# Selective scans: four of sixteen input products per job made by scaling a transposed tile and turning it back (two in layer 1)

## The chip, the core and the metric

The kernel runs on one core of a Trainium2 chip. The metric is the device time of one execution in microseconds, lower is better. A core has five engines that run side by side, each with its own queue of instructions in a fixed order: PE (TensorE: matmuls and transposes, writes to PSUM only), DVE (VectorE), ACT (ScalarE), POOL (GpSimd), and SP, which here issues the DMAs.

## What is computed

The program is four layers on a tensor of 2 images x 56 x 56 positions x 128 channels (L = 3136 positions): two state-space layers, then an attention with a long-filter mixer, then an attention with experts. The change is in the first two, in their selective scans. Cut to what matters:

```python
def step(state, inp):                      # one position after another
    u_i, d_i, b_i, c_i = inp
    dA = jnp.exp(d_i[..., None] * A)       # decay, per channel d and state n (N = 16)
    state = dA * state + (d_i * u_i)[..., None] * b_i[:, :, None, :]
    y = jnp.einsum('bkdn,bkn->bkd', state, c_i)
    return (state, y)
```

There are four directions k: along the rows, along the columns, and both backwards. `delta` d is a softplus of a small projection, B and C are projections as well, the same for all channels. Layer 0 has 256 channels per image, so two tiles of 128 channels, and handles one image after the other. Layer 1 is called for four "heads" in turn with 64 channels per image, so both images share one tile of 128 partitions.

## The kernel before

Class `Scans` (from line 111) does the scans of both layers. The positions are cut into four quarters of 784. A group is one direction and one quarter (16 groups); a job is a group and one channel tile (`ci`); a job has 16 steps, one for each state n. Layer 0 has 32 jobs per image, layer 1 has 16 per head: 2048 steps in all. Channels lie on the partitions, positions along the free dimension, so one step is a handful of 128x784 instructions:

- the decay a = exp(A delta), by ACT into one of two PSUM slots, `pa`, that alternate by step (line 339)
- the input product h = du x B, where du = delta x input (line 223), and B has one row per state that all partitions need. There are two kinds of it. For a pooled state (`POOLED`, five of 16: 2, 5, 8, 11, 14) a DMA broadcasts the row from DRAM to all partitions (line 299, tile `b`), and POOL multiplies (line 433). For the other eleven PE spreads the row with two bf16 matmuls into the single PSUM tile `pb` (line 364), and DVE multiplies (line 417)
- the scan itself by DVE, h = a h_before + h, in place (line 358)
- the product p = h x C by POOL, with C broadcast by DMA (lines 299 and 430)
- the sum over states by PE: matmuls with the identity (layer 1: a centering matrix) that accumulate in PSUM (`add_up`, line 378). A job's accumulation opens with `begin_sum` (line 392) and ends with `take_out` by ACT (line 398).

The order is written out by hand: `emit(s)` issues what belongs to step s, and the scheduler is off (`manual_schedule`). In one `emit(s)`, in this order: decay of step s+1; the state of s-1 saved (`keep`, line 350); DVE's product of s+1; PE's spread for s+2; pieces of preparation at place 0; the scan of s; DMA of B for s+6 and of C for s+3; POOL's p of s, then POOL's product of s+3; the sums; pieces at place 2. The sums are opened when step n = 2 of a job is two steps old; after that each step adds one product, and the steps n = 6, 9 and 12 add two.

The preparation of the next group is cut into pieces, and `preparation` (line 257) says at which step and place each goes: `rows` (projection by PE, copy by ACT), `keep`, `fetch`, `band`, `rest`, `store` and `spread` (B split into three bf16 parts, by way of DRAM), `steps` (delta's projection), `soft` (softplus, which needs another ACT table), `copy` (the input by PE into PSUM, with an identity matmul) and `times` (du by DVE). Pieces of place 0 take the PSUM tile `pb` too. The first group of each run of scans is prepared by `first` (line 230), which is called in the stage before, at the third of its seven chunks.

Tiles h and p have six buffers each, C four, B two.

Of the kernel before, what the change touches and what calls it, by code (L numbers as in the profile page):

```python
# [106 lines left out]
POOLED = (2, 5, 8, 11, 14)  # L107
HALF = QT // 2


class Scans:
# [13 lines left out]
    def __init__(self, k, ctx, nch, row, col, y, w, side=None):  # L125
# [7 lines left out]
        )  # L133

    def begin(self):
        self.groups = []
        for kd in (0, 2, 1, 3):
            back = kd >= 2
            for step, q in enumerate(range(4) if not back else range(3, -1, -1)):
                self.groups.append(dict(kd=kd, q=q, step=step, back=back))  # L140

    def open(self, ctx):
        k, nch = self.k, self.nch
        self.once = ctx.enter_context(k.pool("scan4", 1))
        self.two = ctx.enter_context(k.pool("scan5", 2))
        self.hp = ctx.enter_context(k.pool("scanh", 6))
# [8 lines left out]
    def pieces_of(self, g, once, dram):  # L155
# [60 lines left out]
        def copy(ci, ps):  # L216
            g["copy"] = product(ps, [0, 1], lambda m: k.ident, [xq[ci]])

        def times(ci, copied=True):
# [4 lines left out]

        return dict(
            rows=rows, keep=keep, fetch=fetch, band=band, rest=rest, store=store, spread=spread, steps=steps,
            soft=soft, copy=copy, times=times,
        )

    def first(self, pool):  # L230

        self.begin()
        own = {"xd": self.y[0][:, 0:QT], "whole": self.y[-1][:, QT : QT + QT // 4]}
# [20 lines left out]
        for ci in range(self.nch):  # L254
            f["times"](ci, False)

    def preparation(self, groups, short):
# [15 lines left out]
        if self.nch == 2:  # L273
            lists = [[
                (0, 0, "rows", [0]), (3, 0, "rows", [1]), *bands(5, 8, 11, 2, 16, 19), (12, 0, "steps", 0, [0, 1]),
                (16, 0, "steps", 1, [0, 1]), (20, 2, "soft", 0), (20, 2, "soft", 1), *du(22, 0), *du(25, 1),
            ]]
        elif short:
            lists = [
                [(0, 0, "rows", [0, 1]), *bands(1, 3, 5, 1, 8, 11), (3, 0, "steps", 0, [0, 1]), (10, 2, "soft", 0), *du(12, 0)],  # L280
                [(6, 0, "rows", [0, 1]), *bands(7, 9, 12, 2, 17, 20), (9, 0, "steps", 0, [0, 1]), (10, 2, "soft", 0), *du(16, 0)],
            ]
        else:
            lists = [
                [(0, 0, "rows", [0, 1]), *bands(1, 4, 7, 2, 12, 15), (3, 0, "steps", 0, [0, 1]), (20, 2, "soft", 0), *du(22, 0)],
                [(6, 0, "rows", [0, 1]), *bands(7, 13, 17, 2, 22, 31), (16, 0, "steps", 0, [0, 1]), (20, 2, "soft", 0), *du(25, 0)],
            ]
        at = []
        for g, todo in zip(groups, lists):
            f = self.pieces_of(g, lambda name, n: self.once.tile([128, n], F32, name=name), self.dram)  # L290
# [17 lines left out]
    def all_steps(self):  # L308
# [12 lines left out]
        self.steps = steps  # L321
        for s in range(-6, len(steps) + 4):
# [5 lines left out]
    def prepare(self, s, place):  # L328
        for _, _, f, args in self.pieces.get((s, place), ()):
            if place == 0:  # L330
# [4 lines left out]

    def decay(self, x):
        g, ci = x["g"], x["ci"]
        x["a"] = self.pa[x["s"] % 2].tile([128, 1024], F32, name=f"a{x['s'] % 2}")[:, 0:QT]
# [1705 lines left out]
```

## Time and profile before

| what | value |
|---|---|
| median of 3 runs | 9109.56 us (9106.62 to 9113.72) |
| span of the profiled execution | 9096.6 us, 93496 instructions |
| busy over the span | PE 88%, DVE 78%, ACT 42%, POOL 70% |
| scans of layer 0 | 102.5 to 1359.2 and 1490.9 to 2748.7 us |
| scans of layer 1 | 2883.7 to 3519.5, 3615.9 to 4248.9, 4345.6 to 4983.4 and 5079.7 to 5719.0 us |
| DMA | 1362.92 MB, of it 1024 + 2048 issues of `c<-rows` and 320 + 640 of `b<-rows` |

The shares over the whole span mix stages with different limits, so they are read by stage. This is the picture in 40 slices, one digit per slice, the busy share in tenths:

```
PE   8888888888887888888888888699999999999998
DVE  8999998999997997998999899511467667665442
ACT  4555545555555555554555554433211111114331
POOL 6999996999996997998899799566311111115551
```

The scans are the first 25 slices; the dips in them are the stages between two runs of scans. After them come attention, mixer and experts, which the change does not touch. The time of a run is the span and 13 us around it (9109.56 against 9096.6, the median against one profiled execution).

### The profile page before, as it was taken

The numbers are of one execution on the slowest core, as the hardware profiler recorded it, in microseconds if no ns is written. First come the engines' busy times: TensorE is split into PE (matmuls) and PEld (weight loads), VectorE is DVE, ScalarE is ACT, GpSimd is POOL, SyncE is SP. The second block draws the span as 40 slices with busy tenths as digits, with TensorE's granted clock in tenths as the row PEclk, the third lists the DMA queues.
The fourth block names the chain that finished last, engine by engine and source line by source line (L and its number), as shares of the span: only waits on it lengthen the run. The fifth ranks groups of instructions, "written<-read, shape, count | busy, mean of one in ns | idle before, by whom it ended". The sixth has DMA issues, their size and how long they took to land. (4 is left out here: it accounts for less than half of the span.)

```text
span 9096.6 us, 93496 instructions
## 1 busy us (share of the span) xinstructions
PE 7993.2 (88%) x28687; PEld 4765.5 (52%) x28687; DVE 7088.0 (78%) x7568; ACT 3854.8 (42%) x6644; POOL 6350.1 (70%) x4066
## 2 busy tenths in 40 slices
PE   8888888888887888888888888699999999999998
PEld 4444445444444444444444444355688888874555
DVE  8999998999997997998999899511467667665442
ACT  4555545555555555554554555433211111114331
POOL 6999996999996997998899799566311111115551
PEclk9999999999999998998999899799999999999999
DMA  5666664666664995996898699100233333320004
GB/s 159 221 221 220 222 212 127 221 221 220 222 220 110 230 226 134 227 228 157 203 227 204 157 227 224 39 3 3 85 96 105 104 94 110 93 63 8 14 1 135
DMA packets 780368, 1362.92 MB, mean 150 GB/s; under 512 B 133101, under 2 KB 405486, under 8 KB 779834
## 3 DMA queue, kind: packets, MB, share of 16 engines
q1 hardware_dynamic: 779866, 1356.95, 53.1%
q8 instruction: 227, 3.72, 0.2%
q14 instruction: 275, 2.25, 0.1%
HBM read 1317.03 MB, written 39.60 MB: 149 GB/s over the span
## 5 line engine op out<-in xcount | busy, mean ns | idle before, releaser
L430 POOL TENSOR_TENSOR p<-h,c 128x784 f32<-128x784 f32 x2048 | 3761.2, 1864 | 115.0 <-DVE h L358 33.1
L358 DVE TENSOR_TENSOR_SCAN h<-a,state,h 128x784 f32<-128x784 f32 x1536 | 2791.8, 1840 | 51.6 <-ACT a L339 28.7
L378 PE MATMUL acc<-p,center 128*128 128x392 f32 x4096 | 1499.0, 499 | 22.7 <-POOL p L430 20.8
L378 PE MATMUL acc<-p,ident 128*128 128x392 f32 x4096 | 1491.9, 498 | 6.7 <-POOL p L430 6.7
L417 DVE TENSOR_TENSOR h<-du,b 128x784 f32<-128x784 f32 x1408 | 1336.7, 949 | 75.6 <-PE b L364 70.4
L339 ACT ACTIVATE a<-delta,L0A 128x784 f32<-128x784 f32 x1024 | 939.3, 918 | 973.4 <-DVE h L358 971.5
L339 ACT ACTIVATE a<-delta,L1A 128x784 f32<-128x784 f32 x1024 | 939.2, 917 | 908.3 <-DVE h L358 905.3
L364 PE MATMUL b<-three,sel 96*128 96x512 bf16 (+1 forms) x2816 | 728.6, 341 | 563.9 <-DVE h L417 460.1
L433 POOL TENSOR_TENSOR h<-du,b 128x784 f32<-128x784 f32 x640 | 1190.3, 1860 | 4.1 <-PE pcv L460 4.1
L378 PEld LDWEIGHTS acc<-p,center 128*128 128x128 f32 x4096 | 740.9, 192 | 536.8 <-POOL p L430 60.2
L378 PEld LDWEIGHTS acc<-p,ident 128*128 128x128 f32 x4096 | 743.9, 192 | 512.8 <-POOL p L430 26.5
L1089 POOL TENSOR_TENSOR total<-total,e 128x448 f32<-128x448 f32 (+1 forms) x644 | 735.6, 1142 | 326.0 <-ACT e L1078 286.0
L358 DVE TENSOR_TENSOR_SCAN h<-a,h 128x784 f32<-128x784 f32 x512 | 901.7, 1780 | 36.7 <-ACT a L339 21.1
L364 PEld LDWEIGHTS <-sel 96*128 96x128 bf16 x2816 | 281.5, 100 | 1230.9 <-issue 1048.6
L1572 DVE TENSOR_TENSOR u<-u,cv 128x512 f32<-128x512 f32 x1024 | 623.7, 681 | 326.6 <-PE cv L1559 325.4
L1603 POOL TENSOR_TENSOR u<-u,S 128x1024 f32<-128x1024 f32 x64 | 150.0, 2365 | 1041.0 <-DVE S L1572 1041.0
L1078 ACT ACTIVATE e<-sc 128x448 f32<-128x448 f32 (+1 forms) x700 | 377.2, 543 | 723.0 <-PE sc L1076 596.3
L1574 ACT COPY u<-cv 128x512 f32<-128x512 f32 x256 | 149.5, 587 | 829.3 <-PE cv L1559 775.7
L1673 PE MATMUL pj<-u,Wm 128*128 128x196 f32 (+8 forms) x1536 | 354.7, 384 | 5.7 <-DVE A L1679 5.7
L1076 PE MATMUL sc<-big 128*128 128x448 f32 (+1 forms) x700 | 323.4, 547 | 15.4 <-ACT e L1078 12.3
L1070 PE MATMUL av<-e,big 128*128 128x448 f32 (+1 forms) x700 | 320.9, 545 | 1.2 <-DVE e L1083 1.0
L1653 POOL TENSOR_TENSOR both<-mpm 128x512 f32<-128x512 f32 x32 | 40.6, 1269 | 392.3 <-DVE Wm L1709 272.8
(452 smaller groups left out, 11251.1 us busy)
## 6 DMA issues: line engine op xcount, KB each, us to landing
c<-rows SPq DMA_DIRECT2D x1024, 392.0 KB, 4.0
c<-rows SPq DMA_DIRECT2D x2048, 196.0 KB, 4.8
b<-rows SPq DMA_DIRECT2D x320, 392.0 KB, 4.5
b<-rows SPq DMA_DIRECT2D x640, 196.0 KB, 4.6
H<-raw SPq DMA_DIRECT2D x32, 1568.0 KB, 7.6
wC<-win SPq DMA_DIRECT2D x64, 576.0 KB, 6.4
w<-in_L_weight_dram SPq DMA_DIRECT2D x52, 512.0 KB, 6.3
wA<-win SPq DMA_DIRECT2D x64, 384.0 KB, 5.6
```

The lines of the kernel that those rows point to most:

```text
L339: self.k.nc.scalar.activation(x["a"], g["delta"][ci], AF.Exp, scale=self.w["A"](g["kd"], ci, x["n"]))
L358: self.k.nc.vector.tensor_tensor_scan(h, a, h, start, ALU.mult, ALU.add)
L364: self.k.nc.tensor.matmul(ps[:, c0:c1], lhsT=self.w["selB"](x["n"]), rhs=x["g"]["three"][:, c0:c1], start=True, stop=True)
L378: nc.tensor.matmul(job["acc"][:, i, 0:392], lhsT=self.w["sum"], rhs=x["p"][:, 392 * i : 392 * (i + 1)], start=False, stop=n == NS - 1,)
L417: nc.vector.tensor_tensor(one["h"], one["g"]["du"][one["ci"]], one["b"], ALU.mult)
L430: nc.gpsimd.tensor_tensor(now["p"], now["h"], now["c"], ALU.mult)
L433: nc.gpsimd.tensor_tensor(three["h"], three["g"]["du"][three["ci"]], three["b"], ALU.mult)
L1076: nc.tensor.matmul(ps[:n], lhsT=keys[b][:, KT * j : KT * j + n], rhs=q, start=True, stop=True)
L1078: nc.scalar.activation(e[:n], ps[:n], AF.Exp, scale=scale)
L1089: nc.gpsimd.tensor_tensor(total[:n], total[:n], e[:n], ALU.add)
L1572: nc.vector.tensor_tensor(place(o), place(o), ps, ALU.add)
L1673: nc.tensor.matmul(ps[:, lo - c0 : hi - c0], lhsT=Ws[f][:, eo, r, :], rhs=u[:, b, f, lo - a0 : hi - a0], start=f == 0, stop=f == 1,)
```

## The change

The states of a job are now of three kinds. Pooled are four of 16: 1, 5, 9, 13 in layer 0, and 1, 6, 9, 14 in layer 1. Direct (DVE) are eight in layer 0, ten in layer 1. The third kind is new: turned, 3, 7, 11, 15 in layer 0, and 3, 11 in layer 1.

For a turned state the input product is made in the turned layout, with positions on the partitions. Seven tiles of 112 positions make a quarter (`TS`). There B has one value per partition, so ACT makes the product by a copy with a per-partition scale: `fan`, seven instructions of 112x128 per state in layer 0, and 14 of 112x64 in layer 1, where the two images have different B. They are spread over the four steps s-5 to s-2. Then PE transposes the seven tiles back into the PSUM slot that the state's decay would have taken (`back`), and the scan reads the addend there. The decay of a turned state goes to SBUF instead, into the state's h buffer, one step earlier than the others, and the scan writes over it.

That needs du and B in the turned layout once per group: `turn` (seven transposes of du by PE, one copy by ACT) per channel tile, and `across` (seven transposes of the projections, one copy). `copy` of the preparation is now a copy by ACT into PSUM, not a matmul. The lists of `preparation` are written anew: the pieces that use `pb` go to steps after which no direct state comes, softplus goes to step 17 (9 in the first set of layer 1), and in that set du is made from SBUF without a copy. `first` does the turning for the first group. In layer 1, `hT` of the stage between the scans becomes a small tile of a pool with two buffers, since its old place holds the turned tiles.

```diff
-POOLED = (2, 5, 8, 11, 14)
+TS = QT // TP
...
         def copy(ci, ps):
-            g["copy"] = product(ps, [0, 1], lambda m: k.ident, [xq[ci]])
+            g["copy"] = ps[:, :, 0:HALF]
+            nc.scalar.copy(g["copy"], part(xq[ci], [0, 1]))
...
+        def transposed(out, of, n, tiles, ps):
+            ps = ps.rearrange("p i c -> p (i c)")[:TP]
+            for i, j in enumerate(tiles):
+                nc.tensor.transpose(ps[:, n * i : n * (i + 1)], of[0:n, TP * j : TP * (j + 1)], k.ident[0:n, 0:n])
+            nc.scalar.copy(
+                out[:, tiles[0] : tiles[-1] + 1], ps[:, 0 : n * len(tiles)].rearrange("p (i c) -> p i c", c=n)
+            )
+
+        def across(ps):
+            g["BT"] = once("BT", 32 * TS)[:TP]
+            transposed(g["BT"].rearrange("p (i c) -> p i c", c=32), g["xd"], 32, range(TS), ps)
+
+        def turn(ci, ps, tiles=range(TS)):
+            transposed(g["duT"][ci], g["du"][ci], 128, tiles, ps)
...
         for ci in range(self.nch):
             f["times"](ci, False)
+        f["across"](ps())
+        for ci in range(self.nch):
+            for i in range(0, TS, 3):
+                f["turn"](ci, ps(), range(i, min(i + 3, TS)))
...
-                (0, 0, "rows", [0]), (3, 0, "rows", [1]), *bands(5, 8, 11, 2, 16, 19), (12, 0, "steps", 0, [0, 1]),
-                (16, 0, "steps", 1, [0, 1]), (20, 2, "soft", 0), (20, 2, "soft", 1), *du(22, 0), *du(25, 1),
+                (1, 0, "rows", [0]), (3, 0, "rows", [1]), (5, 0, "across"), *bands(6, 8, 10, 2, 15, 19),
+                (13, 0, "steps", 0, [0, 1]), (15, 0, "steps", 1, [0, 1]), (17, 2, "soft", 0), (17, 2, "soft", 1),
+                *du(21, 0), *du(23, 1), (25, 0, "turn", 0), (31, 0, "turn", 1),
...
-                [(0, 0, "rows", [0, 1]), *bands(1, 4, 7, 2, 12, 15), (3, 0, "steps", 0, [0, 1]), (20, 2, "soft", 0), *du(22, 0)],
-                [(6, 0, "rows", [0, 1]), *bands(7, 13, 17, 2, 22, 31), (16, 0, "steps", 0, [0, 1]), (20, 2, "soft", 0), *du(25, 0)],
+                [
+                    (1, 0, "rows", [0, 1]), *bands(2, 5, 8, 2, 13, 15), (4, 0, "steps", 0, [0, 1]), (7, 0, "across"),
+                    (17, 2, "soft", 0), *du(20, 0), (25, 0, "turn", 0),
+                ],
+                [
+                    (9, 0, "rows", [0, 1]), *bands(10, 14, 20, 2, 25, 31), (15, 0, "steps", 0, [0, 1]),
+                    (17, 2, "soft", 0), *du(23, 0), (28, 0, "across"), (31, 0, "turn", 0),
+                ],
...
+        self.fans = {}
+        for i, x in enumerate(x for x in steps if x["n"] in self.turned):
+            x["bT"] = self.bT[i % len(self.bT)]
+            todo = [(x, j, *part) for j in range(TS) for part in self.w["parts"]]
+            each = -(-len(todo) // 4)
+            for j in range(0, len(todo), each):
+                self.fans.setdefault(x["s"] - 5 + j // each, []).extend(todo[j : j + each])
...
+    def fan(self, x, i, c0, c1, row):
+        g, r = x["g"], 32 * i + row + x["n"]
+        self.k.nc.scalar.activation(
+            x["bT"][:, i, c0:c1], g["duT"][x["ci"]][:, i, c0:c1], AF.Copy, scale=g["BT"][:, r : r + 1]
+        )
+
+    def back(self, x):
+        x["b"] = self.slot(x, 512 - 4 * TP)
+        for i in range(TS):
+            self.k.nc.tensor.transpose(x["b"][:, TP * i : TP * (i + 1)], x["bT"][:, i, :], self.k.ident[:TP, :TP])
...
     def decay(self, x):
         g, ci = x["g"], x["ci"]
-        x["a"] = self.pa[x["s"] % 2].tile([128, 1024], F32, name=f"a{x['s'] % 2}")[:, 0:QT]
+        if x["n"] in self.turned:
+            x["a"] = x["h"] = self.hp.tile([128, QT], F32, name="h")
+        else:
+            x["a"] = self.slot(x)
...
-        if one:
+        if one and one["n"] not in self.turned:
             self.decay(one)
...
         if before:
             self.keep(before)
-        if one and one["n"] not in POOLED:
+        if two and two["n"] in self.turned:
+            self.decay(two)
+        for args in self.fans.get(s, ()):
+            self.fan(*args)
+        if one and one["n"] in self.turned:
+            self.back(one)
+        self.prepare(s, 1)
+        if one and self.direct(one):
             one["h"] = self.hp.tile([128, QT], F32, name="h")
             nc.vector.tensor_tensor(one["h"], one["g"]["du"][one["ci"]], one["b"], ALU.mult)
-        if two and two["n"] not in POOLED:
+        if two and self.direct(two):
             self.spread(two)
```

## The prediction

> **What bounds the kernel now.** First I read the busy shares by stage: the six stretches in which the scans run (1 and 2 are layer 0, one per image, 512 steps each; 3 to 6 are layer 1, one per head, 256 steps each). Columns: length, then busy time of PE, weight load, DVE, ACT, POOL, then granted clock, DMA share, GB/s.
>
> ```profile
> 102.50:1359.20 1256.70, 1049.90 (x3224) 534.27 (x3224) 1227.40 (x892) 655.00 (x1122) 1230.48 (x700) 0.96 0.68 219
> 1490.90:2748.70 1257.80, 1051.52 (x3224) 535.03 (x3224) 1227.64 (x894) 655.73 (x1122) 1230.74 (x701) 0.96 0.69 221
> 2883.70:3519.50 635.80, 526.20 (x1605) 265.26 (x1606) 613.12 (x446) 338.05 (x583) 620.33 (x365) 0.95 0.90 226
> ...
> sum 5060.40, PE 4207.35 PEld 2130.41 DVE 4908.32 ACT 2663.23 POOL 4945.46; mean PE 701.22 PEld 355.07 DVE 818.05 ACT 443.87 POOL 824.24
> ```
>
> The scans are 5060 of the span's 9097 us, and in them DVE and POOL are both busy for 97 to 98%; PE for 83%, ACT for 53%. So two engines bound the scans together, and a change helps only if it takes work from both. Next, the groups of instructions in stage 1, and a stretch of its timeline by engine (start, length, engine, line, count):
>
> ```profile
> L430 POOL TENSOR_TENSOR p<-h,c 128x784 f32<-128x784 f32 x509 | 934.1, 1864 | 26.3 <-PE acc L378 12.1 <-DVE h L358 7.9 <-issue 5.6
> L433 POOL TENSOR_TENSOR h<-du,b 128x784 f32<-128x784 f32 x159 | 296.5, 1865 | 0.0
> ```
> ```profile
> 620.63 0.95 DVE L417 TENSOR_TENSOR h<-du,b 128x784 f32<-128x784 f32 x1
> 621.49 1.84 DVE L358 TENSOR_TENSOR_SCAN h<-a,state,h 128x784 f32<-128x784 f32 x1
> ```
> ```profile
> 618.07 5.45 POOL L430 TENSOR_TENSOR p<-h,c 128x784 f32<-128x784 f32 x3
> ```
> ```profile
> 606.45 1.48 PE L378 MATMUL acc<-p,ident 128*128 128x392 f32 x4
> 607.76 0.50 PE L364 MATMUL b<-three,sel 96*128 96x512 bf16 x2
> 608.10 1.48 PE L378 MATMUL acc<-p,ident 128*128 128x392 f32 x4
> ```
>
> What to see: back to back, a POOL product takes 5.45/3 = 1.81 us, a DVE product 0.86 (621.49 less 620.63), a scan 1.75 (two in a row are 3.59). On PE a sum (four matmuls) takes 1.31 (607.76 less 606.45), a spread of B 0.34. I count by jobs of 16 steps, 32 of them in a layer-0 stage, 16 in a layer-1 stage. Now: POOL 21 x 1.81 + 0.5 ("rest" of the bands; 1.0 in layer 1) = 38.5 (39.0); DVE 16 x 1.75 + 11 x 0.86 + 0.88 (du) = 38.3. A job really takes 1257/32 = 39.3 in layer 0 and 2546/64 = 39.8 in layer 1. So POOL's count explains all but 0.7 of it.
>
> **The change, per job.** The order of instructions after the change confirms the counts: DVE products fall from 1408 to 1152, POOL's from 640 to 512, scans and p stay at 2048.
>
> Layer 0 has 4 pooled, 4 turned, 8 direct states. POOL: 20 x 1.81 + 0.5 = **36.7** (-1.8). DVE: 28.0 + 8 x 0.86 + 0.88 = 35.8. Layer 1 has 4, 2, 10. POOL: 36.2 + 1.0 = 37.2; DVE: 28.0 + 8.6 + 0.88 = **37.5**. A turned scan reads its decay from SBUF and its addend from PSUM, no row shows that; today it is the other way round, at 1.84, and the two-SBUF product of du took 0.97 to 1.34 against 0.96 with one in PSUM. One operand stays in SBUF, so I keep 1.84; 0.1 more on four scans would be within DVE's 0.9 of slack in layer 0.
>
> ACT gets the fans. The row nearest is the final layernorm's scaling:
>
> ```profile
> 5744.54 2.45 ACT L89 ACTIVATE X<-X,stf 112x128 f32<-112x128 f32 x8
> ```
> One of these is 0.39, so back to back (2.45 - 0.39)/7 = 0.29; 28 per job in layer 0 make 8.2. In layer 1 the tiles are 64 wide; the slope between this row and the decay (918 ns at 784) is 0.81 ns per element, so 0.24, and 28 make 6.8. With the copies (0.8 for x, 0.9 for duT, 0.2 to 0.4 for BT) ACT goes from 655/32 = 20.5 to 30.7, and from 21.1 to about 30 in layer 1: 80%. It stays hidden as long as decays, which come first in each step's ACT order, start when the scan that frees their PSUM slot ends; each has a scan and usually a product (2.6 us) for its 0.9. A fan queued ahead delays a decay by at most 1.0. Softplus and its two table loads (1.28 each) block ACT for some 4 us as now; DVE's surplus over POOL in layer 0 absorbs that, in layer 1 it doesn't.
>
> PE gets seven transposes per turned state. The row with their exact shape, and the timeline's four in a row without a wait:
>
> ```profile
> 5768.53 0.95 PE L1145 MATMUL pt<-ident,U 112*128 112x112 f32 x4
> ```
> (0.95 - 0.39)/3 = 0.19, so 1.31 per state and 1.5 until the last result. Against that, three spreads less (1.0) and x's copies gone from PE (1.3). What matters is where it falls. The sums of a job are not spread evenly: add_up runs in 13 of the 16 steps and does 16 sums. In these 13 steps PE has now 16 x 1.31 + 8 x 0.34 + 2.6 (dt or copy matmuls) = 26.3, or 2.03 per step against a period of 2.46. Afterwards: 21.0 + 6 x 0.34 + 3 backs x 1.31 + 2.6 to 3.7 (dt and BT, or two turns) = 29.6 to 30.7, **2.27 to 2.36 per step, against POOL's 36.7/16 = 2.30.** So PE becomes a third full engine there. Each back also adds a wait: it needs the scan two steps earlier done (its PSUM slot); behind it on PE stand the next spread (DVE's product waits) and the sums (POOL's p buffers wait, six of them). Between that scan and the turned scan lie 2.6 us of DVE work, the back needs 1.5 and semaphores, so about 0.9 is spare. The loss this brings lies between 0.7 per job (today's idle, nothing added) and 2.0 (PE's page time 32.8 - 1.5 - 1.4 + 6.1 + 1.5 + 0.6 = 38.1, plus 0.7, less 36.7). I take 1.5: PE's count equals POOL's already without any wait. Layer 0: 38.2, or -1.1 x 64 = **-70**. In layer 1 the 13 steps have one back, some 28.5 or 2.19 per step against 2.35: PE isn't full, but DVE and POOL are level. I take 1.0 over DVE's 37.5, 38.5: -1.3 x 64 = **-83**.
>
> The Trainium skill ("TensorE: Matmul & The Clock Gate", Part 4: PE-mode transpose) speaks against the change: it gives a 128x128 transpose about 275 ns in a kernel, where the trace has 187 in a row. By 275 a back would take 1.9, the 13 steps 2.4 to 2.5 each, and layer 0 would gain nothing; the trace's row decides here.
>
> Outside the scans: the preparation of the first group (six times) gets 21 transposes in layer 0, 14 in layer 1, and their copies, and the middle stages are led by PE (119 of 132 us busy, 84 of 96). Lower end: PE's 0.19 each, 2 x 4 + 4 x 2.7 = 19. Upper end: PE also waits from the last dt matmul to du (4 us in the trace), and for each copy in between (two psum buffers, some 0.7 each round): 2 x 12 + 4 x 9 = 60. The order after the change puts other matmuls between the transposes in most of them, so I take **+30**, near the lower end. The smaller hT tile has its copy and readers in the same chunk: nothing.
>
> DMA: 192 broadcasts less of 4032 (50 MB of 1357). In layer 1 the queues are at 0.90; bytes per job fall by 5%, the time by 3%, so that stays. On SP the preparation's own DMAs move by one to three steps, and none past the step that needs its data.
>
> Sum: -70 - 83 + 30 = -123, 9097 - 123 = 8974 in the profiled execution. The median of the runs shown, 9110, is 13 above that span: **8987**.
>
> **Rivals.**
> 1. POOL and DVE as bounds with today's idle, PE hidden by buffers. For it: today's PE waits for DVE's products (125 us in stage 1), and spaced direct states end that wait. Against it: the 13-step count. Layer 0 37.4, layer 1 38.2: -122 - 102 + 20 = -204, **8906**.
> 2. PE bounds layer 0: its page time, 38.1, plus 0.7 = 38.8 (-32), layer 1 38.6 (-77), middles at +48: -61, **9049**. For it: it already holds up DVE now and then (9.7 us "PE b" in stage 1). Against it: the page time counts tails that overlap.
> 3. Slower: the back comes late for its scan. If PE is still at sums (1.31 each, waiting for p) when the slot comes free, the spare 0.9 goes and DVE stands before every turned scan. At 1.0 us each: DVE 35.8 + 4 + 0.7 = 40.5 (+77), layer 1 37.5 + 2 + 0.7 = 40.2 (+26), +30: +133, **9243**. It decides from about 0.9 us of lateness on, and breaks even at some 0.65 us each (64 x (36.5 + 4x - 39.3 + 38.2 + 2x - 39.8) + 30 = 0). Against it: DVE runs up to three steps ahead of POOL, so part of a stall is made up.
>
> That the change doesn't do what it says is ruled out by the counts.
>
> **Chances.** Forecast 0.44, rival 1 0.20, rival 2 0.22, rival 3 0.14. Range 8890 to 9120: from below rival 1 to past no change; it leaves out most of rival 3. A measurement can't tell less than 0.2% (18 us) from no change: faster 0.79 (rival 3 gone, and a part of rival 2's spread), same 0.06, slower 0.15.
>
> **What would show it.** Stage 1 at about 1222 us with POOL 96% busy, PE at 95% or more, DVE idle before scans named "PE a" (the transposes); layer-1 stages at 616. DVE at 95% and POOL at 98% with PE waits gone speaks for rival 1; idle POOL naming "PE acc" for rival 2; over 30 us of DVE idle per stage before turned scans for rival 3. Middles longer by 10 each would show my +30 too small. A fan far from 0.29, a transpose from 0.19, or a scan from 1.84 would break the sums.

## The result, and the profile after

| kernel | median us | runs | ratio to before, 95% interval |
|---|---|---|---|
| before | 9108.9 (9106.6 to 9113.7) | 4 | |
| changed | 9229.8 (9223.8 to 9238.5) | 4 | 1.013 (1.0116 to 1.0145) |

The change costs 121 us; forecast was a gain of 122. The profiled executions differ by 131.9 us (9228.5 less 9096.6), 11 more than the medians. In every execution on record with both numbers the time is about 2 us above the span (changed: 9230.39 for a span of 9228.5). So the 13 us between the median and the span of the kernel before are not something around the span: its one profiled execution was some 11 us faster than its median. The split by stage, with the forecast beside it, compares these two executions:

| part | before | after | difference | forecast |
|---|---|---|---|---|
| two layer-0 stages | 2514.5 | 2514.9 | 0 | -70 |
| four layer-1 stages | 2545.9 | 2610.9 | +65 | -83 |
| six stretches ahead of the scans | 658.6 | 724.1 | +65 | +30 |
| all behind the last scan | 3377.6 | 3378.6 | +1 | 0 |

Read first the busy times by stage in the changed kernel. The columns are those of the prediction's first fence: length, then busy time of PE, weight load, DVE, ACT, POOL, then granted clock, DMA share, GB/s.

```profile
109.20:1369.40 1260.20, 1094.53 (x4123) 619.75 (x4123) 1148.62 (x797) 955.94 (x2091) 1176.47 (x668) 0.94 0.68 209
2924.60:3576.60 652.00, 551.41 (x1952) 300.29 (x1952) 602.83 (x430) 463.16 (x1062) 594.51 (x349) 0.93 0.81 211
...
sum 5125.80, PE 4393.69 PEld 2439.87 DVE 4708.27 ACT 3763.60 POOL 4733.40; mean PE 732.28 PEld 406.65 DVE 784.71 ACT 627.27 POOL 788.90
```

The work moved as counted. In stage 1 POOL is busy for 1176 us instead of 1230, DVE for 1149 instead of 1227, ACT for 956 instead of 655. Yet the stage is as long as before. No engine is full any more: POOL 93%, DVE 91%, PE 87%. So the time is in waits. The groups of stage 1 name them (behind the second bar: idle time of the engine ahead of the group, and what ended it), first in the kernel before, then in the changed one:

```profile
L358 DVE TENSOR_TENSOR_SCAN h<-a,state,h 128x784 f32<-128x784 f32 x384 | 698.4, 1841 | 10.6 <-ACT a L339 9.5 <-POOL h L433 1.0
L417 DVE TENSOR_TENSOR h<-du,b 128x784 f32<-128x784 f32 x350 | 332.5, 950 | 10.7 <-PE b L364 9.1
L223 DVE TENSOR_TENSOR du<-delta,b 128x784 f32<-128x784 f32 x30 | 28.8, 958 | 2.7 <-PE b L166 1.7
```
```profile
L516 POOL TENSOR_TENSOR p<-h,c 128x784 f32<-128x784 f32 x511 | 940.3, 1864 | 83.8 <-DVE h L437 36.4 <-PE acc L457 26.9 <-issue 17.3
L437 DVE TENSOR_TENSOR_SCAN h<-a,state,h 128x784 f32<-128x784 f32 x288 | 521.0, 1834 | 18.5 <-ACT a L417 18.4
L503 DVE TENSOR_TENSOR h<-du,b 128x784 f32<-128x784 f32 x255 | 243.3, 954 | 63.8 <-PE b L443 57.6 <-POOL p L516 6.2
L437 DVE TENSOR_TENSOR_SCAN h<-h,state,a 128x784 f32<-128x784 f32 x96 | 176.7, 1840 | 0.0
L231 DVE TENSOR_TENSOR du<-delta,b 128x784 f32<-128x784 f32 x30 | 28.8, 959 | 20.8 <-ACT b L225 20.8
```

DVE waits in three places: 57.6 us before direct products, for PE's spread of B (L443; 9.1 us before the change); 28.4 before scans, for ACT's decays (18.4 here, 10.0 in a second group; 13.1 in the same two groups before); 20.8 before the product for du, for ACT's copy of the input (L225; new). Before the turned scans, `h<-h,state,a`, it waits for nothing: the transposes are in time. POOL's p then waits for DVE's h, and for PE's sums to give back p's buffers.

Where the spread is late can be seen in the timeline of a turned state in layer 1 (start, length, engine, line, and in brackets the idle time ahead of it):

```profile
3955.98 0.83 PE L443 MATMUL b<-three,sel 96*128 96x512 bf16 x2 [2.38 <-DVE du L231]
...
3961.28 1.48 PE L457 MATMUL acc<-p,center 128*128 128x392 f32 x4
...
3962.59 0.84 PE L406 MATMUL a<-ident,big 112*128 112x112 f32 x7
...
3963.27 0.50 PE L443 MATMUL b<-three,sel 96*128 96x512 bf16 x2
...
3963.80 0.97 DVE L503 TENSOR_TENSOR h<-du,b 128x784 f32<-128x784 f32 x1 [1.75 <-PE b L443]
3964.69 1.84 DVE L437 TENSOR_TENSOR_SCAN h<-h,state,a 128x784 f32<-128x784 f32 x1
...
3966.66 1.85 POOL L516 TENSOR_TENSOR p<-h,c 128x784 f32<-128x784 f32 x1 [2.53 <-DMA c<-rows]
```

PE does what its queue says: sums, then the seven transposes (L406), then the spread (L443). DVE's queue has it the other way round: first the direct product of the state after the turned one, which needs the spread, and behind it the turned scan, which needs the transposes. So the transposes that nobody needs yet hold up the spread by 0.68 us (3962.59 to 3963.27). DVE stands for 1.75 us. The rest is not the order: PE had stood for 2.38 us until DVE's product for du freed the one tile `pb`, and from 3955.98 on it works without a pause. POOL, whose next p needs the scan that ended at 3966.53, stands for 2.53 us. The profile puts that wait down to a DMA, but it ends 0.13 us behind the scan.

### The profile page after: what moved, and what is told of

It is laid out like the page before. It is cut to its first block, busy times and chain, and to the rows that moved or that the text cites. A ratio compares the mean times of both kernels' runs of the same rounds, so it can differ in the third digit from the quotient of the medians.

```text
span 9228.5 us, 103426 instructions
## 1 busy us (share of the span) xinstructions
PE 8232.9 (89%) x31951; PEld 5110.1 (55%) x31951; DVE 6887.0 (75%) x7312; ACT 4982.6 (54%) x10580; POOL 6137.6 (67%) x3938
## 5 line engine op out<-in xcount | busy, mean ns | idle before, releaser
L437 DVE TENSOR_TENSOR_SCAN h<-a,state,h 128x784 f32<-128x784 f32 x1248 | 2255.5, 1835 | 44.4 <-ACT a L417 44.3
L503 DVE TENSOR_TENSOR h<-du,b 128x784 f32<-128x784 f32 x1152 | 1097.9, 953 | 291.8 <-PE b L443 266.2
L417 ACT ACTIVATE a<-delta,L1A 128x784 f32<-128x784 f32 x896 | 820.0, 916 | 554.1 <-DVE h L437 551.9
L519 POOL TENSOR_TENSOR h<-du,b 128x784 f32<-128x784 f32 x512 | 948.8, 1853 | 2.1 <-PE pcv L546 2.1
L417 ACT ACTIVATE a<-delta,L0A 128x784 f32<-128x784 f32 x768 | 702.1, 914 | 340.6 <-DVE h L437 331.2
L443 PE MATMUL b<-three,sel 96*128 96x512 bf16 (+1 forms) x2304 | 588.9, 337 | 297.7 <-DVE h L503 158.1
L437 DVE TENSOR_TENSOR_SCAN h<-a,h 128x784 f32<-128x784 f32 x416 | 729.9, 1776 | 30.5 <-ACT a L417 30.0
L1670 ACT COPY u<-cv 128x512 f32<-128x512 f32 x256 | 149.5, 587 | 827.5 <-PE cv L1655 774.2
L395 ACT ACTIVATE X<-X,BT 112x128 f32<-112x128 f32 x1680 | 587.1, 392 | 0.0
L443 PEld LDWEIGHTS <-sel 96*128 96x128 bf16 x2304 | 222.6, 100 | 650.1 <-issue 389.2
L437 DVE TENSOR_TENSOR_SCAN h<-h,state,a 128x784 f32<-128x784 f32 x288 | 530.1, 1841 | 0.0
L395 ACT ACTIVATE big<-big,BT 112x64 f32<-112x64 f32 x1680 | 449.8, 335 | 0.0
```

Source lines behind the costliest of these rows:

```text
L395: self.k.nc.scalar.activation(x["bT"][:, i, c0:c1], g["duT"][x["ci"]][:, i, c0:c1], AF.Copy, scale=g["BT"][:, r : r + 1])
L417: self.k.nc.scalar.activation(x["a"], g["delta"][ci], AF.Exp, scale=self.w["A"](g["kd"], ci, x["n"]))
L437: self.k.nc.vector.tensor_tensor_scan(h, a, b, start, ALU.mult, ALU.add)
L443: self.k.nc.tensor.matmul(ps[:, c0:c1], lhsT=self.w["selB"](x["n"]), rhs=x["g"]["three"][:, c0:c1], start=True, stop=True)
L503: nc.vector.tensor_tensor(one["h"], one["g"]["du"][one["ci"]], one["b"], ALU.mult)
L519: nc.gpsimd.tensor_tensor(three["h"], three["g"]["du"][three["ci"]], three["b"], ALU.mult)
```

## Theories

**Order**: in PE's queue the transposes (`back`) stand ahead of the spread, though DVE wants the spread first. **Load**: ACT has 300 us more to do in a layer-0 stage, and its decays and copies come late. **Places**: the pieces of preparation stand at steps where their engines are backed up. For the stretches ahead of the scans: the turning in `first`, or the granted clock. They don't exclude each other; the runs were to give each its share.

## Experiments

Each is timed beside the kernel before on one chip. The kernel before had medians of 9110.9 us in the set with experiments 1 to 4, 9114.0 with 5 to 8, 9110.3 with 9 and 10, 9117.1 with 11 and 12, and 9112.9 with 13 to 15, so a difference between two sets can be off by up to 7 us. The changed kernel's 9230 is the reference unless said otherwise.

### 1. The spread ahead of the transposes

```diff
-        if one and one["n"] in self.turned:
-            self.back(one)
         self.prepare(s, 1)
...
         if two and self.direct(two):
             self.spread(two)
+        if one and one["n"] in self.turned:
+            self.back(one)
         self.prepare(s, 0)
```

> TensorE is issued the spread of the second next scan (for VectorE's next product) ahead of the seven transposes of the next turned scan, not behind them. Order theory (the added time is VectorE waiting for a spread that stands behind the transposes): VectorE's waits at the product L503 for the spread fall from about 57 us to under 35 in a layer-0 scan stage, the two layer-0 stages shorten by 15 to 20 us each and the four of layer 1 by 5 to 10 each; 9160 to 9180 us against 9230 of the changed kernel. Load theory (ScalarE is too full and its copies and decays come late): no change, 9220 to 9240.

Measured: **9148**, ratio 1.0036 (1.0023 to 1.0049): 82 us less. Layer-0 stages 1240.3 and 1240.7 (20 and 14 less), layer-1 stages 639 to 642 (10 to 14 less). The groups of stage 1:

```profile
L516 POOL TENSOR_TENSOR p<-h,c 128x784 f32<-128x784 f32 x510 | 936.4, 1864 | 65.6 <-DVE h L437 38.8 <-PE a L406 13.3 <-issue 10.9
L501 DVE TENSOR_TENSOR h<-du,b 128x784 f32<-128x784 f32 x255 | 242.9, 952 | 41.3 <-PE b L443 40.0 <-issue 0.2
```

The order theory holds, in layer 0 with the size it gave, in layer 1 and in all with more (82 us; 50 to 70 were expected). The wait for the spread fell to 40 us, not below 35; most of what is left sits at step 16 of each set of 32 (1.85 us a set), where the spread stands behind a `steps` product and a doubled sum. There PE is busy without a pause (10.80 us of the 10.80 from 526.8 to 537.6), so at such steps it is PE's load that delays DVE. The waits for ACT did not move (52 us).

### 2. Nothing turned ahead of the scans

All sixteen states of the first group are direct or pooled; `first` turns nothing. Pieces of the first set of 32 steps stand elsewhere, since the PSUM tile is then taken at other steps.

```diff
-        f["across"](ps())
-        for ci in range(self.nch):
-            for i in range(0, TS, 3):
-                f["turn"](ci, ps(), range(i, min(i + 3, TS)))
...
+    def turns(self, x):
+        return x["n"] in self.turned and x["g"] is not self.groups[0]
```

> Nothing is turned in the middles: the first of the sixteen quarter sets is scanned with direct products only, so neither the rows nor the products of the first set are transposed before the scans begin. If the turning in the middles is what made them 65 us longer in all: the six stretches ahead of the scans lose 45 to 60 us together, the first set gives back 2 to 3 us per stage (twice that in layer 0), 9180 to 9205 us. If it is the place of the normed rows (a rotating buffer in place of a whole image) or the clock: the middles lose under 15 us together, 9220 to 9245.

Measured: **9206**, 24 us less. The six stretches take 670.1 us instead of 724.1: 54 less, as the turning theory said. Five of them are back at the length of before (103.4, 130.6, 95.6, 95.4, 95.7), which is 46 of the 54. But the scans gave back 30 (16 to 24 were expected): in layer 0 the first 32 steps take 86.5 us instead of 79.6 and 78.5. The third stretch stayed long (149.5), with nothing turned in it.

### 3. The copy by TensorE, as before

```diff
-            g["copy"] = ps[:, :, 0:HALF]
-            nc.scalar.copy(g["copy"], part(xq[ci], [0, 1]))
+            g["copy"] = product(ps, [0, 1], lambda m: k.ident, [xq[ci]])
```

> The copy of the rows for the scaled input goes back to TensorE's product with the identity, as before; all else is the changed kernel. Load theory (ScalarE's copies come late): the waits on that copy (21 us in a layer-0 stage, 6 in one of layer 1) go, 15 us per layer-0 stage and 4 per layer-1 stage, about 9185 us. Order theory: TensorE's queue gets 5.9 us more in a set of 32 steps, and what ScalarE no longer delays, the queue does: 9225 to 9255 us.

Measured: **9226**, 4 us less, within the spread of the runs. DVE's wait for the copy in stage 1 only changed its name: 27.1 us for PE's matmuls in place of 20.8 for ACT's copy. Moving the late piece to another engine brought nothing here: both are behind at that step.

### 4. One fan of seven

```diff
-            self.fan(*args)
+            if args[1] == 0:
+                self.fan(*args)
```

> Of the seven tiles of ScalarE's input products of a turned scan only the first is made; the other six keep what the buffer held, so the output is not the reference's. ScalarE loses some 215 us of busy time in a layer-0 stage, TensorE nothing. Load theory: the waits on ScalarE (decay and copy, 50 us in a layer-0 stage) fall by over half, 25 to 35 us per layer-0 stage and 10 per layer-1 stage, about 9130 us. Order theory: under 10 us per layer-0 stage, 9200 to 9230 us.

The kernel leaves out six of the seven tiles of every turned product; the order of its instructions is otherwise the same.

Measured: **9112**, 118 us less. Layer-0 stages 1221.1, 36 less each on average; layer-1 stages 642, 10 less each. The groups of stage 1:

```profile
L437 DVE TENSOR_TENSOR_SCAN h<-a,state,h 128x784 f32<-128x784 f32 x288 | 521.1, 1834 | 4.2 <-ACT a L417 3.7
L504 DVE TENSOR_TENSOR h<-du,b 128x784 f32<-128x784 f32 x255 | 243.7, 956 | 61.6 <-PE b L443 58.8 <-POOL p L517 2.7
L231 DVE TENSOR_TENSOR du<-delta,b 128x784 f32<-128x784 f32 x30 | 28.8, 959 | 3.5 <-ACT b L225 3.2
```

DVE's wait for decays fell from 28.4 to 8.1 us and for the copy from 20.8 to 3.2, while the wait for the spread stayed (58.8). So with the pieces at these steps ACT's load is a cause of its own, at least as large as the order, and the two act at different waits (the twelfth kernel carries the whole load again and waits less). It also says what the forecast had wrong: 80% busy was not hidden.

### 5. No copy

The first experiment, and the product for du reads the input from SBUF.

```diff
-            return [(at, 0, "copy", ci), (at, 2, "times", ci)]
+            return [(at, 2, "times", ci, False)]
```

> The first experiment (spread ahead of the transposes, 9148 us) and in it no copy of the rows at all: VectorE's product for the scaled input reads them from SBUF, as 16 of the 128 such products of the changed kernel do already (0.975 us against 0.972 with the copy). Load theory (ScalarE's late copies hold VectorE): the wait for the copy (21 us in a layer-0 stage, 7 in one of layer 1) goes and the decays behind it come earlier: 15 to 20 us per layer-0 stage, 4 to 6 per layer-1 stage, 9090 to 9105 us. Rival (ScalarE is late there from the softplus and its table loads, not from the copies): the wait moves to the next decay or spread, 9135 to 9150 us.

Measured: **9192**, 44 us more than the first experiment. Neither theory held. The group says why (duration in ns: least, median, most); first the changed kernel, where only the first sets read from SBUF, then this one:

```profile
L231 DVE TENSOR_TENSOR du<-delta,b x112: 944/971/972, 163.5 to 5787.8; 128x784 f32<-128x784 f32 x112
L231 DVE TENSOR_TENSOR du<-delta,big x16: 967/976/2151, 56.2 to 5267.2; 128x784 f32<-128x784 f32 x16
```
```profile
L231 DVE TENSOR_TENSOR du<-delta,big x128: 946/1750/2646, 57.6 to 5743.7; 128x784 f32<-128x784 f32 x128
```

With one operand in PSUM the product never exceeds 0.97 us; with both in SBUF it takes between 0.95 and 2.65, 1.75 in the median. POOL's p takes 1902 ns in the mean of stage 1 instead of 1864 in the first experiment, so both sides pay. The 0.976 of the changed kernel's 16 products was a median: the trace has four of them at 2.15 us, one in each layer-1 stage, and the two at the start, where no scan runs yet, at 0.976.

The Trainium skill ("SBUF — State Buffer", SBUF: two separate sides) states the rule: VectorE with two SBUF inputs and a GpSimd instruction that reads SBUF share a port pair that one holds for a whole instruction while the other blocks. This run agrees: the worst product, 2.65 us, starts at 5256.19, 0.03 behind a POOL product that ends at 5258.00, and ends 0.84 behind it; POOL's next p then takes 2.56 us.

### 6 to 8. Pieces at other steps, without the copy

The sixth is the fifth with another list for layer 0 (below) and one made by the same rules for layer 1. The seventh keeps the very first turned state direct and turns the first group's input at steps -1 and 9. The eighth is the sixth with the transposes ahead of the spread again.

```diff
-                (1, 0, "rows", [0]), (3, 0, "rows", [1]), (5, 0, "across"), *bands(6, 8, 10, 2, 15, 19),
-                (13, 0, "steps", 0, [0, 1]), (15, 0, "steps", 1, [0, 1]), (17, 2, "soft", 0), (17, 2, "soft", 1),
-                *du(21, 0), *du(23, 1), (25, 0, "turn", 0), (31, 0, "turn", 1),
+                (1, 0, "rows", [0]), (3, 0, "rows", [1]), (17, 0, "across"), *bands(6, 8, 10, 2, 15, 19),
+                (7, 0, "steps", 0, [0, 1]), (13, 0, "steps", 1, [0, 1]), (21, 2, "soft", 0), (21, 2, "soft", 1),
+                *du(23, 0), *du(25, 1), (27, 0, "turn", 0), (29, 0, "turn", 1),
```

> The last one, and in it the pieces of preparation stand at other steps: the step-size products at 7 and 13 (layer 1: 7 and 17) and not right behind a begin of a sum or a double addition on TensorE; the softplus at 21 (layer 1: 25), behind the copy of the result and ahead of a turned scan, whose decay is made early. Place theory (the waits stand at steps 16, 20 and 21 of layer 0 and 5, 20 and 26 of layer 1 because pieces queue there): of the 4.5 us waited at these steps in a set of 32 some half goes, 30 to 40 us per layer-0 stage and 8 to 12 per layer-1 stage against the first experiment: 9040 to 9070 us. Rival (TensorE and ScalarE are too full, and waits only move to other steps): within 10 us of the last one.

> The last one, and in it the very first turned scan of each run is done by the direct product, and the input of the first set is turned after the scans have begun, not in the middles. If turning in the middles is what lengthens them (as the second experiment says: 54 us shorter without), 45 to 55 us less than the last one, at a cost of 1 us per stage in the scans. If the place of the turning matters and not its presence (TensorE and ScalarE then do it beside the first scans and delay those): under 20 us less.

> Pieces at other steps and no copy, as two experiments up, but the spread again behind the seven transposes as in the changed kernel. Order and place as separate causes: what the first experiment gained (80 us) is lost again, 9120 to 9150 us. If the late pieces alone were the cause, and the order only mattered because TensorE ran late from them: within 25 us of the one with the order turned as well.

Measured: **9215**, **9209** and **9276**. The sixth and eighth missed by over 120 us, since they were reckoned before the fifth had shown the price of the missing copy. In the sixth, DVE's waits in stage 1 fell from 86 us in the fifth to 40, but its busy time rose from 1163 to 1212: the SBUF product now took 3.06 us in the median of that stage and up to 6.2 in the whole run, nearly three POOL products in a row. So the fall of the waits doesn't show the place theory: the ninth experiment has them again. The seventh came out 6 us below the sixth, not 45 to 55. It took 45 us from the stretches ahead of the scans (668.1 for 712.6) and gave 46 back in the scans, as the second had given back half: where the turning of the first group stands matters little. The eighth is 61 us slower than the sixth: the order has its price here too.

### 9. Pieces at other steps, with the copy

The layer-0 list of the sixth; a similar one in layer 1; the copy by ACT is back everywhere.

> Spread ahead of the transposes, pieces at other steps, and the rows again copied to PSUM ahead of the product (also in layer 1's first sets, where the changed kernel reads them from SBUF). Without the copy that product took 1.2 to 1.75 us in the median and up to 6.2, not 0.97, beside a busy GpSimd. Place theory: the waits of VectorE stay at the 36 to 39 us per layer-0 stage that the kernel without the copy showed (93 in the first experiment), its busy time falls back from 1212 to 1148 us: 1195 to 1210 us per layer-0 stage, 630 to 638 per layer-1 stage, 9030 to 9070 us in all. Rival (ScalarE's copies are late wherever they stand, and the shorter waits were only hidden in the stretched product): 1230 to 1240 per layer-0 stage, 9130 to 9160 us.

Measured: **9166**, 18 us more than the first experiment. The layer-0 stages are 6 and 9 us shorter than there, not 35, and near the rival's 1230 to 1240. DVE's waits in stage 1 are back at 85 us (93 in the first experiment), so most of their fall in the sixth was hidden in the stretched product. One line of stage 1 tells where they are:

```profile
L231 DVE TENSOR_TENSOR du<-delta,b 128x784 f32<-128x784 f32 x30 | 29.1, 971 | 40.5 <-ACT b L225 40.5
```

The decay wait is nearly gone (6.3 us), the copy wait has doubled: the copy at step 23 stands two steps behind softplus and its two table loads (4.3 us). In layer 1 the new list is worse in its first two sets (97 us for the first 32 steps, 86 in the first experiment).

### 10 to 12. Layer 1 as before, the copies later

The tenth is the ninth with nothing turned in layer 1 and the lists of the kernel before there (copy by ACT). The eleventh also moves layer 0's copies, the twelfth puts softplus back to 17. The diff is that of the twelfth against the ninth, without layer 1's lists.

```diff
-                (7, 0, "steps", 0, [0, 1]), (13, 0, "steps", 1, [0, 1]), (21, 2, "soft", 0), (21, 2, "soft", 1),
-                *du(23, 0), *du(25, 1), (27, 0, "turn", 0), (29, 0, "turn", 1),
+                (7, 0, "steps", 0, [0, 1]), (13, 0, "steps", 1, [0, 1]), (17, 2, "soft", 0), (17, 2, "soft", 1),
+                *du(25, 0), *du(27, 1), (29, 0, "turn", 0), (31, 0, "turn", 1),
...
-            "pooled": (1, 6, 9, 14),
-            "turned": (3, 11),
+            "pooled": (2, 5, 8, 11, 14),
+            "turned": (),
```

> As the last one in layer 0; in layer 1 nothing is turned: direct and pooled products and the pieces at the steps of the kernel before (the copy by ScalarE). If turning two of sixteen states in layer 1 costs more than it brings (its stages went from 636 to 653 us and the stretch ahead of them from 96 to 105): its stages take 633 to 640 us and 96 us ahead of them, so 40 us less than the last one if that has 640 us per stage, 10 if it has 632. If turning pays there too once the order and the places are right: over 10 us more than the last one.

> The last kernel (layer 1 as before, layer 0 with the order and places changed, 9093 us), and in layer 0 the copies and the products for the scaled input at steps 25 and 27, the turns at 29 and 31: not two but four steps behind the softplus. In that kernel VectorE waited 2.33 us for the copy at step 23 and 0.35 at 25, in a set of 32 steps (42 us of its 82 idle in a stage). Place theory: 25 to 35 us per layer-0 stage go, 9025 to 9050 us. Rival (ScalarE is late by a softplus whose 4.3 us nothing hides, and the next decay or spread waits in place of the copy): within 15 us of 9093.

> The one above with the softplus of layer 0 back at step 17, where the changed kernel has it, two steps ahead of the copy of the result. If its place makes the waits (behind it ScalarE has the copy of the result, which TensorE's next sum waits for, and a decay in PSUM): step 20 waits 1.5 us a set again, 20 to 30 us per layer-0 stage more than the one above. If only the distance from the softplus to the copies matters: within 8 us per stage.

Measured: **9093** (0.9981, 0.9970 to 0.9991), **9044** (0.9922, 0.9908 to 0.9935) and **9039** (0.9916, 0.9902 to 0.9929). All three beat both kernels, the tenth barely. The tenth gained 73 us on the ninth and not 40, since the ninth's layer-1 stages had been 647 to 650 us. Layer 1 put back takes 636 to 640 us per stage and 95 to 97 ahead of the last three, as before. The copies two steps later took 18 and 24 us from the layer-0 stages, a little less than said; DVE's wait for them in stage 1 fell from 42 to 7.5 us. With the copies at 25 and 27, softplus at 17 or 21 makes no difference that counts (9039 and 9044): its own place was not the cause. Its distance to the copy alone was not either. The changed kernel has four steps between them (17 and 21) and waits 20.8 us, the eleventh has four (21 and 25) and waits 7.5. What the copy waits for is all that ACT has in front of it, as the changed kernel's timeline shows:

```profile
544.81 1.28 ACT L221 ACT_TABLE_LOAD   x1
546.10 1.60 ACT L221 ACTIVATE delta<-delta 128x784 f32<-128x784 f32 x2
...
548.40 1.28 ACT L417 ACT_TABLE_LOAD   x1
...
555.56 0.81 ACT L225 COPY b<-big 128x784 f32<-128x784 f32 x1
...
556.40 0.97 DVE L231 TENSOR_TENSOR du<-delta,b 128x784 f32<-128x784 f32 x1 [1.28 <-ACT b L225]
```

From 540.30 until the copy at 555.56 ACT never pauses: behind softplus it has decays, fans and the copy of a result to do. With the copy four steps later, in the twelfth, the wait is 4.9 us. Stage 1 of the twelfth kernel, first by stage, then its groups:

```profile
108.80:1316.60 1207.80, 1077.99 (x4123) 612.09 (x4123) 1148.69 (x797) 955.13 (x2091) 1174.93 (x668) 0.96 0.71 218
...
3560.60:4196.60 636.00, 511.52 (x1545) 256.78 (x1546) 613.34 (x446) 348.38 (x598) 621.49 (x366) 0.94 0.90 223
```
```profile
L505 POOL TENSOR_TENSOR p<-h,c 128x784 f32<-128x784 f32 x511 | 938.4, 1867 | 32.9 <-DVE h L426 18.7 <-PE a L395 3.6 <-issue 3.0
...
L490 DVE TENSOR_TENSOR h<-du,b 128x784 f32<-128x784 f32 x255 | 243.6, 955 | 36.9 <-PE b L432 32.4 <-POOL h L508 2.6 <-POOL whole L202 0.8
...
L231 DVE TENSOR_TENSOR du<-delta,b 128x784 f32<-128x784 f32 x30 | 28.8, 960 | 4.9 <-ACT b L225 4.9
```

DVE, ACT and POOL are busy to 2 us as in the changed kernel (1148.7, 955.1, 1174.9), PE to 17, and the stage is 52 us shorter, 49 shorter than before the change. POOL is 97% busy. Turning in layer 0 pays with this order and these places.

### 13 to 15. Each part alone

The thirteenth is the twelfth with the transposes ahead of the spread; the fourteenth is the changed kernel with only layer 1 put back; the fifteenth is the twelfth with layer 1 turned as in the change (spread first).

> The fastest kernel so far (9039 us: layer 1 as before, layer 0 with the spread first and the copies later), and in it the spread again behind the seven transposes. Order theory: VectorE's waits for the spread come back as they went (57 to 40 us a stage in the first experiment, where the stages lost 14 to 20 us): 15 to 20 us per layer-0 stage, 9070 to 9080 us. If the order mattered only because TensorE was late from badly placed pieces: under 5 us per stage, 9037 to 9050 us.

> The changed kernel with layer 1 alone put back (nothing turned there, pieces at the steps of before, the copy by ScalarE); layer 0 as changed, with none of what the experiments mended. If layer 1's loss is its turning (stages 653 for 636 us, the stretches ahead of the last three 105 for 96): 4 times 14 to 17 and 3 or 4 times 8 us less than 9230: 9130 to 9150 us. If a third of that loss came from outside layer 1's own scans (the granted clock): 9155 to 9180 us.

> The fastest kernel so far, and layer 1 turned as in the changed kernel, with the spread first. Its stages and the stretches ahead of them are then those of the first experiment (640 us and 105): 4 times 2 and 3 or 4 times 8 to 9 us more than 9039, so 9065 to 9080 us, if layer 1's loss is the filling of the turned way at the start of each stage and not what is saved in the steady part. If turning pays in layer 1 with layer 0 mended: under 9039.

Measured: **9090** (51 more than the twelfth), **9149** (81 less than the changed kernel) and **9085** (47 more than the twelfth). The thirteenth's layer-0 stages are 1236.2 and 1234.1, 28 and 27 longer (15 to 20 were expected), and the wait is the one that the order theory names:

```profile
L492 DVE TENSOR_TENSOR h<-du,b 128x784 f32<-128x784 f32 x255 | 244.2, 958 | 62.1 <-PE b L432 59.8 <-POOL p L505 1.3 <-issue 0.3
```

So the order costs in layer 0 whatever the places are. The fourteenth has layer-0 stages of 1256.9 and 1254.5, as changed, layer-1 stages of 636 to 641 (653), and 95 to 97 us (105) ahead of the last three: layer 1 alone makes two thirds of the 121. The rest, 40 us, lies in the first three stretches (38 us longer than before in the profiles); the layer-0 stages are 3 us shorter than before. In the fifteenth the last three stretches are 104 to 106 us and the layer-1 stages 639 to 643. From the 33rd step on they take 554 us on average, the twelfth's 553, the changed kernel's 563.5. So with the order right turning neither costs nor saves in layer 1's steady part, and its fill (9 us ahead of each stage, 2 in the first 32 steps) is the loss.

## Why the prediction was wrong, step by step

- **The counts of POOL and DVE: right.** Busy times fell by 54 and 79 us in stage 1; the counts had said 58 and 80. **The fans' rate and the scan with its decay in SBUF: right** (0.29 and 0.24 us apart, 1.84 us).
- **"(0.95 - 0.39)/3 = 0.19, so 1.31 per state and 1.5 until the last result": the transposes' size was wrong.** Seven take 0.84 us in the scans (the timeline above) and hold up what follows by 0.68; they start 0.10 apart. The row of 0.19 came from a stretch in which the kernel before had half its clock; the window over that row shows it in the last columns, granted clock 0.50:

```profile
5765.00:5770.00 5.00, 1.65 (x7) 1.30 (x7) 4.39 (x8) 1.53 (x3) 0.00 (x0) 0.50 0.00 0
```

  Before a duration is taken from a row, the row's clock has to be read. The 275 ns that the Trainium skill ("TensorE: Matmul & The Clock Gate", Part 4: PE-mode transpose) gives for one of 128x128 in bf16 was weighed as a distance from start to start. Here (112x112, fp32) the length of one is 259 ns in the median and the distance 100, so the figure is near the length and far from the rate.
- **"PE becomes a third full engine": wrong.** PE went from 84 to 87% of stage 1 with 166 us idle. With 0.68 for a back the prediction's own count of the 13 steps gives at most 21.0 + 2.0 + 2.0 + 3.7 = 28.7, or 2.21 per step against 2.30 (an estimate): not full. The loss that this step was to price (1.5 us of idle per job) came, but not in this way: PE delays DVE by the order of its queue, and by its load only at single steps (step 16 in experiment 1).
- **The idle per job, 1.5 in layer 0 and 1.0 in layer 1, carried the forecast and failed.** Measured: 1260.2/32 less 36.7 is 2.7 in layer 0, 2610.9/64 less 37.5 is 3.3 in layer 1. I had seen that "behind it on PE stand the next spread (DVE's product waits)" and then priced only a full queue. Shown in its place: the order of back and spread (experiment 1: 14 to 20 us per layer-0 stage, 10 to 14 per layer-1 stage; 13: 27 to 28 per layer-0 stage), and late pieces on ACT (10 to 12: 18 to 24 us per layer-0 stage for the copies alone). A second tile `pb`, for which PE waits 32 us of stage 1 until du is done, was not tried.
- **"It stays hidden" (ACT at 80%): wrong by 36 us per layer-0 stage** (experiment 4). **"DVE's surplus over POOL in layer 0 absorbs that" (the softplus): wrong**; DVE waited 49 us for ACT in stage 1, 13 before the change. Yet it is not the share that decides: the twelfth kernel has the same 955 us on ACT and 22 us of such waits. The copy was put on an engine that at this step was still behind from a softplus, and DVE's queue has the product that needs it ahead of its scans.
- **Layer 1, -83: wrong in sign.** 81 us of loss go when only layer 1 is put back (14). About 10 us per stage were the order (the steady part: 563.5 in the changed kernel, 554 in the fifteenth), the rest the fill.
- **The stretches ahead of the scans, +30: too small by half.** 54 of the 65 are the turning (experiment 2), which is near the upper end that I had worked out (60, with PE's waits for du and for each copy) and far from the lower one (19, the transposes alone); its terms were not taken apart. The rest is the third stretch: 135.0 us in the one profile of the kernel before, 141 to 157 in all others, even with nothing turned in it. PE's granted clock was 0.90 there before and 0.75 after, and 0.76 to 0.88 in the other profiles; why is open. Since that one execution was 11 us faster than the median, part of this rest may belong to that execution and not to the change; no run shows which.
- **DMA nothing, and the tail: right.**
- **Rival 3** gave 9243 and came near the time, but by another mechanism: DVE hardly ever waited for the transposes (0.3 us in stage 1 of experiment 1, none in the changed kernel). "Over 30 us of DVE idle per stage before turned scans" would have rejected it; the idle lay before direct products. **Rival 1** had 37.4 us per job in layer 0; the twelfth kernel reaches 1207.8/32 = 37.7.

What stays open: why turning, with DVE 11 and POOL 27 us less busy per stage, saves nothing in layer 1's steady part. In the fifteenth POOL's idle time there (44 us before p) is split among DVE's scans, the DMA of C and PE's sums; none was tried alone.

## What to carry to other kernels

When work for a later consumer goes into an in-order queue, put it behind the work that the next consumer needs first, and compare the two queues instruction by instruction: seven transposes of 0.84 us in front of a spread of 0.34 cost 28 us in a stage with PE 12% idle. A piece behind a block of 4.3 us on its engine needs enough steps for that engine to catch up, or less in front of it: DVE's wait for the copy fell from 42 to 7.5 us with the copy two steps later (10 and 11), and from 20.8 to 3.2 with one fan of seven (4). A new scheme that needs a fill should be tried first where the stage is long: here it brought 50 us per stage of 1257 and lost 10 per stage of 636.

## What the hardware showed besides

PE's clock falls in the middle of a busy stage. In the changed kernel PE idled for 1.06 and 2.13 us with 0.49 of work in between; then four 128x392 matmuls took 2.94 us, where four sums of that shape take 1.48. First the timeline of PE, then the window over these matmuls (the last three columns are granted clock, DMA share, GB/s):

```profile
3983.77 0.49 PE L443 MATMUL b<-three,sel 96*128 96x512 bf16 x2 [1.06 <-DVE h L503]
3986.39 2.94 PE L173 MATMUL b<-xd,dt 128*128 128x392 f32 x4 [2.13 <-DVE h L503]
```
```profile
3986.46:3989.88 3.42, 3.42 (x6) 1.84 (x7) 3.38 (x2) 0.54 (x2) 3.42 (x3) 0.50 0.84 244
```

After these waits of PE 3.42 us at half clock follow. By stage it is small (0.94 in stage 1 for 0.96 before and in the twelfth kernel). Here it stretched work that DVE was to need while the queues were already late; how often that happens was not counted.
